# Dense pieces of elements 2 and 3 in halves, pieces spread by their length, and maxima twelve units ahead

## The chip, the cores and the metric

The kernel runs on one core of one Trainium2 chip. The metric is the device time of one execution in microseconds, from three executions of each kernel; lower is better. A separate execution was profiled, and every duration below comes from that one.

## The reference

Four elements of 1024 tokens with 256 channels pass through two layers. Each layer is attention and then a feed-forward part, and after each of the four there is a residual sum and a layer norm:

```python
x = _layernorm(x + _L0_attn_ref(x, ...))   # 16 heads of 16, q and k normalised and rotated, no mask
x = _layernorm(x + _L0_ffn_ref(x, ...))    # silu(x Wg^T) * (x Wu^T), then Wd; 768 hidden
x = _layernorm(x + _L1_attn_ref(x, ...))   # 8 heads of 32, causal
x = _layernorm(x + _L1_ffn_ref(x, ...))    # 16 experts, top 2, capacity 512
```

All matrix products are in float32. Both softmaxes subtract the row's maximum. For the first attention this is done as

```python
attn = jnp.einsum('bqhd,bkhd->bhqk', q, k)
attn = jax.nn.softmax(attn, axis=-1)
out = jnp.einsum('bhqk,bkhd->bqhd', attn, v)
```

## The kernel before

**Stages.** TensorE (PE) works through one long list of instructions whose order is written by hand. After a start-up part come: the first attention of element 0, the first attention of element 1, the second attention of element 0, the first attention of element 2, the second attention of element 1, the first attention of element 3, the second attentions of elements 2 and 3, and then the experts.

**The first attention in units.** The 16 heads of an element are four groups of four. A group has 16 units. In each unit `Attend.head` makes the scores of four heads (four matmuls of 32 rows that run side by side in the array, PE line 491), ScalarE (ACT) takes their exponential (line 500), and `Attend.values` multiplies the exponentials of the unit before with the values (PE line 509, "av"). The row maxima that the exponentials need are made one group ahead by `Maxima.head`: four more matmuls per unit (PE line 467), each reduced by VectorE (DVE, line 470). So `first_units` pairs unit i of group n with maxima unit i of group n+1: sixteen units ahead. Sixteen units of maxima of the very first group run alone, before the first attention of element 0 starts, and in the last group of element 3 there are no maxima left to pair with.

The eight score and maximum matmuls are issued as two fours, two of each kind in a four, and each needs one of the six PSUM banks of the pool `ps_s`. A bank comes free when ACT has taken its exponential or DVE has reduced it. The order on PE within a unit is: first four, the values of the unit before, for some units a transpose "pt" or "pto" of the heads' tiles, second four, and then the unit's place for other work.

**The other work.** `weave(units, n, pieces, ...)` puts a list of pieces into these places: the feed-forward part of layer 0 (`ffn0`), the projections for the second attention (`project1`), the output projections (`out_project0`, `out_project1`), the router (`route`). All of them write one PSUM bank, the only buffer of the pool `ps_m` (tag "m"), when `weave` is called with `big=False`, as it is in all first attentions; the "pt" and "pto" transposes use that bank too. In the second attentions `big=True`, and the pieces share the six banks of `ps_s`.

Before the change every piece counts alike: with 54 entries in the 64 units of element 2 an entry is issued where its number is due. Most dense pieces fill a whole bank, with eight matmul instructions of 256 columns (each product of two blocks is four matmul calls of two instructions). Shorter and longer ones are: a turn (four transposes), a router product "pl" (eight short instructions) and a down projection "dn" (twelve instructions). `second_end(b)` lists the output projection and router of element b, with entries `wait` that do nothing, so that some units stay empty there. Behind these come the rest of the feed-forward part and `project1`.

**Beside PE.** The bank of a piece is emptied as follows: a turn by one ACT copy of 512 columns (line 640), `gate_up` by an ACT tanh (664) and two DVE operations (665, 666), an output projection by two DVE additions in `add_residual` (556), `project1` by ACT copies (931, 935). Work with a delay (`later`) and the routing steps of `dispatch` are put on DVE and GpSimd (POOL) at the end of a unit, behind that unit's reductions and ahead of its piece. `dispatch` starts at unit 26 of the first attentions of elements 2 and 3, one step per unit.

Of the kernel before, what the change touches and what calls it, by code (L numbers as in the profile page):

```python
# [10 lines left out]
F32 = mybir.dt.float32  # L11
# [8 lines left out]
P = 128  # L20
# [6 lines left out]
FF0 = 768  # L27
# [8 lines left out]
def postln_layers_kernel(ctx: ExitStack, tc: tile.TileContext, a: dict, out: bass.AP):  # L36
# [75 lines left out]
    with ExitStack() as main:  # L112
# [179 lines left out]
        def project_v(b):  # L292
            def piece(j, big):
                xin = take_xin(b, j, "v") if b else xin0[j]
                ps = bank(f"v0_{b}_{j}", big)
                for i in range(2):
                    for c in range(2):
                        nc.tensor.matmul(
                            ps[:, i * 256 : (i + 1) * 256],
                            xin[:, c, i * P : (i + 1) * P],  # L300
                            w0[:, c, 512:768],
                            start=c == 0,
                            stop=c == 1,
                        )
                if b and xin_next:
                    load_ahead()
                nc.scalar.copy(va0[:, 2 * j : 2 * j + 2, :, 0:D0], ps.rearrange("p (t h d) -> p t h d", t=2, h=H0))

            return [lambda big, j=j: piece(j, big) for j in range(4)]

# [234 lines left out]

        def wait(big):
            pass

        mvs, rrs, open_rows = {}, {}, set()
# [33 lines left out]

        def project_out(b, j, oT, w, name, big):

            ps = bank(f"pp{name}_{b}_{j}", big)
            for i in range(2):
                for c in range(2):
                    nc.tensor.matmul(  # L589
                        ps[:, i * 256 : (i + 1) * 256], oT(c, i), w[:, c, :], start=c == 0, stop=c == 1  # L590
                    )
            for i in range(2):
                add_residual(b, 2 * j + i, ps[:, i * 256 : (i + 1) * 256], name)

        def out_project0(b):
# [21 lines left out]
            for h in range(2):  # L617
                out += [lambda big, h=h, c=c: turn(h, c, big) for c in range(2)]
                out += [lambda big, j=j: project(j, big) for j in (2 * h, 2 * h + 1)]
            return out  # L620

        def out_project1(b):


            def project(j, big):
                project_out(b, j, lambda c, i: oT1[b][:, c, (2 * j + i) * P : (2 * j + i + 1) * P], w1o, "a1", big)

            out = [lambda big, j=j: project(j, big) for j in range(4)]
            return out

# [12 lines left out]
        def ffn0(b):  # L643
# [4 lines left out]

            def gate_up(j, f, big):
                if f == 0:  # L650
                    hT[j] = act.tile([P, FF0 // P, 256], F32, tag="hT", bufs=1, name=f"hT_{b}_{j}")
                ps = bank(f"gu_{b}_{j}_{f}", big)
                for i, w in enumerate((wg, wu)):
                    for c in range(2):
                        nc.tensor.matmul(  # L655
                            ps[:, i * 256 : (i + 1) * 256],
                            w[:, c, f * P : (f + 1) * P],
                            xT[j][:, c, :],
                            start=c == 0,
                            stop=c == 1,  # L660
                        )

                sg = act.tile([P, 256], F32, tag="sg", bufs=1, name=f"sg_{b}_{j}_{f}")
                nc.scalar.activation(sg, ps[:, 0:256], AF.Tanh, scale=0.5)
                nc.vector.scalar_tensor_tensor(sg, sg, 1.0, ps[:, 0:256], ALU.add, ALU.mult)
                nc.vector.tensor_tensor(hT[j][:, f, :], ps[:, 256:512], sg, ALU.mult)

# [11 lines left out]

            out = [lambda big: turn(0, big)]  # L680
            for j in range(4):
                out += [lambda big, j=j, f=f: gate_up(j, f, big) for f in range(FF0 // P)]
                if j < 3:
                    out.append(lambda big, j=j: turn(j + 1, big))
                out += [lambda big, j=j, i=i: down(j, i, big) for i in range(2)]
            return out
# [9 lines left out]
        def route(b):  # L696
# [27 lines left out]
            tu, lo = [[lambda big, j=j, f=f: f(j, big) for j in range(4)] for f in (turn, logits)]  # L724
            return tu, lo

# [183 lines left out]
        def project1(b):  # L910
# [9 lines left out]

            def piece(j, s, big):
                ps = bank(f"p1_{b}_{j}_{s}", big)
                for i in range(2):
                    for c in range(2):
# [5 lines left out]
                if s == 2:  # L930
                    nc.scalar.copy(va1[b][:, 2 * j : 2 * j + 2, :].rearrange("p t c -> p (t c)"), ps)
                else:
                    for g in range(G1):
                        to = (qTs, kTs)[s][b, g][:, j * 256 : (j + 1) * 256]
                        nc.scalar.copy(to, ps[:, g * 256 : (g + 1) * 256])

            out = []
            for j in range(4):
                out.append(lambda big, j=j: turn(j, big))
                out += [lambda big, j=j, s=s: piece(j, s, big) for s in range(3)]  # L940
            return out
# [130 lines left out]

        groups = {}
        oq0, oT1, ends = {}, {}, {}

        def first_units(b):
# [3 lines left out]
            for g in range(G0):  # L1080
                n = 4 * b + g
                at = Attend(groups[n], oq0[b])
                mx = groups.get(n + 1)
                for i in range(16):
                    for hp in range(2):

                        then = []
                        for j in range(2):
                            if mx is not None:
                                then += [at.head(i, 2 * hp + j), mx.head(i, 2 * (1 - hp) + j)]  # L1090
                            elif hp == 0:
                                then += [at.head(i, 2 * j), at.head(i, 2 * j + 1)]
                        for fn in then:
                            fn()
                        if hp == 0:
                            if i > 0:
                                at.values(i - 1)
                            elif last is not None:
                                last.values(15)
                            if i == 3:  # L1100
                                groups[n].turn(0, 1, name="a")
                            if i == 5 and last is not None:
                                last.unload(1)
                            if i == 10 and mx is not None:
                                mx.turn(0, 0, name="a")
                            if i == 11:
                                at.unload(0)
                            if i >= 12 and n + 2 in groups:
                                groups[n + 2].turn((i - 12) // 2, i % 2)
                    if i == 0:  # L1110
                        groups[n].close(1)
                    if i == 3 and n + 2 < G0 * B:
                        nb, ng = divmod(n + 2, G0)
                        groups[n + 2] = Maxima(nb, ng)
                    if i >= 4 and n + 2 in groups:
                        groups[n + 2].rotate(4)
                    if i == 8 and mx is not None:
                        mx.close(0)
# [9 lines left out]
        def second_units(b):  # L1128
# [37 lines left out]
            at[last[0]].values(last[1])  # L1166

        def weave(units, n, pieces, big, mid=(), at=0, side=(), side_at=0, rate=1):


            mid, side = list(mid), list(side)
            done, total = 0, len(pieces) + len(mid)
            for u, _ in enumerate(units):
# [4 lines left out]
                if u >= at and mid:  # L1178
                    mid.pop(0)(big)
                    done += 1  # L1180
                    continue
                left = len(pieces)
                while left and (done < total * (u + 1) // n):
                    pieces.pop(0)(big)
                    done, left = done + 1, left - 1
            for piece in pieces:
# [112 lines left out]

        for k, i in enumerate((0, 2, 4, 6, 1, 3, 5, 7, *range(8, 16))):  # L1300
            for red in [groups[0].head(i, h) for h in range(4)]:
# [10 lines left out]
            if k == 10:  # L1312
                groups[0].turn(0, 0, name="a")
            if k >= 12:
                groups[1].turn((k - 12) // 2, k % 2, big=True)
            if 8 <= k < 12:
                second.pop(0)(True)
            else:
                early.pop(0)(False)
# [14 lines left out]

        def second_end(b):
            tu, lo = route(b)
            out = [wait] * 3 + out_project1(b) + [wait, tu[0], wait]
            return out + [lo[0], tu[1], wait, lo[1], tu[2], wait, lo[2], tu[3], wait, lo[3]]

# [10 lines left out]
        for b in (1, 2):  # L1350
# [10 lines left out]
                64,  # L1361
                second_end(b - 1) + ffn[cut:] + project1(b),
                False,
                [lambda big, b=b: load_heads(b + 2, 0)] if b + 2 < B else (),
                30,
                dispatch(b - 1, False),
                26,
            )
# [262 lines left out]
```

## Time and profile before

| | us |
|---|---|
| median of three executions | 2437.87 (2421.68 to 2438.58) |
| profiled execution, its own time | 2424.9 |
| its span, first to last instruction | 2423.2 |
| PE busy | 2300.8 (95% of the span) |
| DVE busy | 1380.2 (57%) |
| ACT busy | 1019.7 (42%) |
| POOL busy | 737.5 (30%) |

Busy times of PE overlap nothing but weight loads, but the ends of its matmuls are modelled, so a busy PE can still be waiting; the distance from one start to the next says more. In the rows of groups, a line stands for engine, source line, operation, tiles and shapes, count, busy time in us, mean ns of one, and the idle time of the engine before it with what ended it. In rows of the timeline the first two numbers are the start in us from the beginning of the span and the length.

### The profile page before, as it was taken

To read this page: it belongs to the slowest core of one execution; us is meant where nothing else is said; L and a number is where in the kernel's file an instruction comes from. 1 tells how busy PE (TensorE), PEld (TensorE's weight loads), DVE (VectorE), ACT (ScalarE), POOL (GpSimd) and SP (SyncE) were. 2 spreads that over 40 slices of the span, in tenths; PEclk is the share of its full clock that TensorE was granted. 3 is DMA by queue.
4 is the path that set the end of the run, shared out by engine and by line. 5 is a ranking of instruction groups with operands and counts; after the bars stand their busy time and mean duration, and the time that the engine had idled before them with its cause. 6 is when DMAs were issued, how large, how long until landed. Compare 5 with 4: busy or idle time off the path is not lost.

```text
span 2423.2 us, 36155 instructions
## 1 busy us (share of the span) xinstructions
PE 2300.8 (95%) x14004; PEld 1138.6 (47%) x14004; DVE 1380.2 (57%) x3231; ACT 1019.7 (42%) x2039; POOL 737.5 (30%) x1101
## 2 busy tenths in 40 slices
PE   8999999999999999999999999999999985999994
PEld 5333334444444443444444434445556443666662
DVE  7766766666557476776674767717645774111113
ACT  2565665555543445545434555562332331111112
POOL 5335337223205143253241420211112153222223
PEclk9999999999999999999999999998999886999997
DMA  3234111000000000000100000112000012444434
GB/s 104 62 120 138 59 59 51 1 28 1 1 28 1 1 1 24 5 27 27 54 1 1 1 1 12 36 46 80 1 1 1 1 58 92 96 107 107 106 88 150
DMA packets 78125, 107.78 MB, mean 44 GB/s; under 512 B 8832, under 2 KB 67200, under 8 KB 76288
## 3 DMA queue, kind: packets, MB, share of 16 engines
q1 hardware_dynamic: 48592, 73.34, 9.3%
q0 software_dynamic: 9984, 14.82, 3.2%
q10 hardware_dynamic: 19376, 17.30, 2.3%
q8 instruction: 110, 1.80, 0.3%
q14 instruction: 63, 0.52, 0.1%
HBM read 66.54 MB, written 38.90 MB: 44 GB/s over the span
## 4 chain that ended last, share of the span: by engine, by line
PE 87%; DVE 8%; DMA 1%; issue 1%; ACT 1%; POOL 1%; SPq 0%; DVEq 0%; POOLq 0%; ACTq 0%
PE sc L491 21%; PE av L509 10%; PE ph L1492 7%; PE py L1508 7%; PE gu L655 7%; PE mx L960 5%; PE sc L1010 4%; PE mx L467 4%; PE p L929 4%; PE dn L671 3%; PE av L1047 3%; PE ppa L589 3%; PE dn L1047 2%; DVE masked L970 2%; PE qk L321 2%; PE pt L458 1%
## 5 line engine op out<-in xcount | busy, mean ns | idle before, releaser
L470 DVE TENSOR_REDUCE part<-mx 128x1 f32<-128x512 f32 x1024 | 655.6, 684 | 305.8 <-PE mx L467 300.8
L500 ACT ACTIVATE pe<-sc 128x512 f32<-128x512 f32 x1024 | 554.2, 596 | 392.4 <-PE mx L467 349.2
L467 PE MATMUL mx<-kT,qT 32*128 32x512 f32 x2048 | 621.6, 637 | 0.2 <-DVE part L470 0.2
L491 PE MATMUL sc<-qT,kT 32*128 32x512 f32 x2048 | 604.3, 637 | 0.0
L491 PEld LDWEIGHTS sc<-qT,kT 32*128 32x128 f32 x2048 | 176.0, 183 | 218.3 <-issue 174.5
L509 PE MATMUL av<-pe,va 128*32 128x512 f32 x2048 | 272.9, 605 | 0.0
L1021 ACT ACTIVATE pe<-sc 128x512 f32<-128x512 f32 (+3 forms) x384 | 157.3, 496 | 202.2 <-PE sc L1010 202.0
L467 PEld LDWEIGHTS mx<-kT,qT 32*128 32x128 f32 x2048 | 186.1, 183 | 33.3 <-issue 16.0
L970 DVE CUSTOM_DVE_ANT_0 masked<-mx,mask_w 128x128 bf16<-128x128 f32 (+3 forms) x256 | 125.4, 490 | 111.7 <-PE mx L960 82.0
L1492 PE MATMUL ph<-dmT,f 128*128 128x512 f32 x384 | 170.4, 602 | 6.8 <-DVE dmT L100 3.5
L1500 ACT ACTIVATE hTm<-ph,b 128x512 f32<-128x512 f32 x96 | 60.8, 684 | 262.2 <-PE ph L1492 262.2
L1508 PE MATMUL py<-f,hTm 128*128 128x256 f32 x768 | 167.7, 379 | 0.0
L1512 POOL DMA_INDIRECT acc_d<-yo,dm x48 | 74.6, 1554 | 287.0 <-DVE yo L1510 243.8
L1508 PEld LDWEIGHTS py<-f,hTm 128*128 128x128 f32 x768 | 145.9, 190 | 25.0 <-issue 5.7
L1024 POOL TENSOR_SCALAR_AFFINE_SELECT pe<-pe 128x256 f32<-128x256 f32 x128 | 51.7, 412 | 313.2 <-ACT pe L1021 311.5
L960 PE MATMUL mx<-kT,qT 32*128 32x512 f32 (+3 forms) x768 | 138.6, 578 | 3.4 <-DVE x L556 2.7
L1509 DVE TENSOR_TENSOR yo<-py,b 128x256 f32<-128x256 f32 x48 | 20.4, 425 | 213.1 <-PE py L1508 213.1
L386 POOL TENSOR_TENSOR ss<-ss,neg_half 128x16 f32<-128x16 f32 x48 | 139.3, 2910 | 0.5
L509 PEld LDWEIGHTS av<-pe,va 128*32 128x32 f32 x2048 | 40.4, 108 | 192.5 <-issue 186.4
L1010 PE MATMUL sc<-qT,kT 32*128 32x512 f32 (+3 forms) x768 | 123.7, 550 | 5.2 <-ACT pe L1021 1.5
L1492 PEld LDWEIGHTS ph<-dmT,f 128*128 128x128 f32 x384 | 72.9, 192 | 97.4 <-issue 86.8
L856 POOL DMA_INDIRECT disp_d<-row,si x48 | 48.4, 1009 | 221.6 <-DVE row L845 215.4
(350 smaller groups left out, 2992.7 us busy)
## 6 DMA issues: line engine op xcount, KB each, us to landing
f<-in_fc SPq DMA_DIRECT2D x14, 1024.0 KB, 5.0
f<-in_fc ACTq DMA_DIRECT2D x10, 1024.0 KB, 5.9
disp_d<-empty ACTq DMA_DIRECT2D x12, 520.0 KB, 3.3
xink<-in_xT SPq DMA_DIRECT2D x24, 256.0 KB, 3.0
qk_d<-xs SPq DMA_DIRECT2D x6, 1024.0 KB, 5.1
xr<-qk_d SPq DMA_DIRECT2D x6, 1024.0 KB, 6.0
dm<-disp_d SPq DMA_DIRECT2D x11, 520.0 KB, 3.6
x<-in_x SPq DMA_DIRECT2D x32, 128.0 KB, 2.7
```

The source lines that it names most:

```text
L467: nc.tensor.matmul(sc, self.qT[r, t * P : (t + 1) * P], self.kT[r, u * 512 : (u + 1) * 512], start=True, stop=True)
L470: return lambda: nc.vector.tensor_reduce(self.part[:, t, u, h : h + 1], sc, AX.X, ALU.max, negate=True)
L491: nc.tensor.matmul(sc, self.m.kT[r, kt * P : (kt + 1) * P], self.m.qT[r, qb * 512 : (qb + 1) * 512], start=True, stop=True)
L500: nc.scalar.activation(self.pes[i, h // 2][:, h % 2, :], sc, AF.Exp)
L509: nc.tensor.matmul(self.av[32 * h : 32 * h + 32, :], va0[:, kt, 4 * self.g + h, :], self.pes[i, h // 2][:, h % 2, :], start=kt == 0, stop= ...
L655: nc.tensor.matmul(ps[:, i * 256 : (i + 1) * 256], w[:, c, f * P : (f + 1) * P], xT[j][:, c, :], start=c == 0, stop=c == 1,)
L960: nc.tensor.matmul(scs[h][:, :n], qT[r, t * P : (t + 1) * P], kT[r, u * 512 : u * 512 + n], start=True, stop=True,)
L970: nc.vector.tensor_tensor_reduce(masked[:, :n], scs[h][:, :n], mask_w[:, 512 - n :], -1.0, -NEG, ALU.add, ALU.min, part)
L1010: nc.tensor.matmul(scs[h][:, off:], ones_h[r, :] if w else kT[r, kt * P : (kt + 1) * P], (self.m.nmT if w else qT)[r, q], start=w == 0, st ...
L1021: nc.scalar.activation(pe[:, j, off:], scs[2 * hp + j][:, off:], AF.Exp)
L1492: nc.tensor.matmul(ph[:, i * CAP : (i + 1) * CAP], f1[:, c, (f + i) * P : (f + i + 1) * P], dmT[:, c, :], start=c == 0, stop=c == 1,)
L1508: nc.tensor.matmul(py[:, :C], hT[:, f, c * P : (c + 1) * P], f2[:, f, :], start=f == 0, stop=f == FF1 // P - 1)
```

## The change

1. Pieces get a cost: 2 for a whole dense piece, 1 for a half, 3 for a down projection, 0.75 for a turn or a router product. `weave` spreads them by cost in place of number, over all its calls that have pieces of such costs: the first attention of element 1 and the second attentions too. The element that loads heads no longer takes a piece's place.
2. `project_out`, `gate_up` and `project1`'s `piece` can be done in halves (`whole`, `in_halves`): one half makes 256 columns of the bank, with four matmul instructions, and is emptied on its own. Only `second_end` asks for halves, so only the first attentions of elements 2 and 3 have them. The entries `wait` are gone there; halves of the feed-forward part stand between the steps of the output projection and the router.
3. `LEAD = 12`: the maxima are twelve units ahead. Twelve units of maxima run alone at the start, and the last four of a group are paired with the first four units of its own attention. The turns and rotations that belong to a maxima unit move with it.
4. `dispatch` starts at unit 25.

The new places on PE in the first attention of element 2: 74 pieces in 64 units, 16 units with two pieces and 6 with none. Before: 46 pieces, one unit with two and 19 with none. For element 3: before 18 units without a piece (2 of them among the 16 units without maxima), after 6, and 18 units in whose place more than one user of the bank follows another, 5 of them among the 12 units without maxima (there the "pto" and "pt" transposes stand in the same place as the pieces).

```diff
+        def whole(fn, *args):
+            def piece(big):
+                fn(*args, big, (0, 1))
+            piece.halves = [lambda big, k=k: fn(*args, big, (k,)) for k in range(2)]
+            piece.cost = 2.0
+            return piece
+
+        def in_halves(pieces):
+            return [h for p in pieces for h in getattr(p, "halves", [p])]
...
-            def gate_up(j, f, big):
+            def gate_up(j, f, big, ks):
...
-                ps = bank(f"gu_{b}_{j}_{f}", big)
-                for i, w in enumerate((wg, wu)):
+                ps = bank(f"gu_{b}_{j}_{f}_{ks[0]}", big)
+                for i in ks:
...
-                sg = act.tile([P, 256], F32, tag="sg", bufs=1, name=f"sg_{b}_{j}_{f}")
-                nc.scalar.activation(sg, ps[:, 0:256], AF.Tanh, scale=0.5)
-                nc.vector.scalar_tensor_tensor(sg, sg, 1.0, ps[:, 0:256], ALU.add, ALU.mult)
-                nc.vector.tensor_tensor(hT[j][:, f, :], ps[:, 256:512], sg, ALU.mult)
+                if 0 in ks:
+                    sgs[j] = sg = act.tile([P, 256], F32, tag="sg", bufs=1, name=f"sg_{b}_{j}_{f}")
+                    nc.scalar.activation(sg, ps[:, 0:256], AF.Tanh, scale=0.5)
+                    nc.vector.scalar_tensor_tensor(sg, sg, 1.0, ps[:, 0:256], ALU.add, ALU.mult)
+                if 1 in ks:
+                    nc.vector.tensor_tensor(hT[j][:, f, :], ps[:, 256:512], sgs[j], ALU.mult)
...
+        LEAD = 12
...
                 at = Attend(groups[n], oq0[b])
-                mx = groups.get(n + 1)
                 for i in range(16):
+                    k, j = divmod(16 * n + i + LEAD, 16)
+                    mx = groups.get(k)
                     for hp in range(2):
                         then = []
-                        for j in range(2):
+                        for h in range(2):
                             if mx is not None:
-                                then += [at.head(i, 2 * hp + j), mx.head(i, 2 * (1 - hp) + j)]
+                                then += [at.head(i, 2 * hp + h), mx.head(j, 2 * (1 - hp) + h)]
...
-            done, total = 0, len(pieces) + len(mid)
+            done, total = 0.0, sum(map(cost, pieces))
...
                 if u >= at and mid:
                     mid.pop(0)(big)
-                    done += 1
-                    continue
-                left = len(pieces)
-                while left and (done < total * (u + 1) // n):
-                    pieces.pop(0)(big)
-                    done, left = done + 1, left - 1
+                while pieces and done + cost(pieces[0]) / 2 < total * (u + 1) / n:
+                    piece = pieces.pop(0)
+                    piece(big)
+                    done += cost(piece)
...
-        for k, i in enumerate((0, 2, 4, 6, 1, 3, 5, 7, *range(8, 16))):
+        for k, i in enumerate((0, 2, 4, 6, 1, 3, 5, 7, *range(8, LEAD))):
...
-        def second_end(b):
+        def second_end(b, fill):
             tu, lo = route(b)
-            out = [wait] * 3 + out_project1(b) + [wait, tu[0], wait]
-            return out + [lo[0], tu[1], wait, lo[1], tu[2], wait, lo[2], tu[3], wait, lo[3]]
+            o, f = in_halves(out_project1(b)), in_halves(fill)
+            out = o[:2] + f[:1] + o[2:4] + f[1:2] + o[4:6] + f[2:3] + o[6:] + f[3:5]
+            for j in range(4):
+                out += [tu[j], f[5 + j], lo[j]]
+            return out + f[9:]
...
-                second_end(b - 1) + ffn[cut:] + project1(b),
+                second_end(b - 1, ffn[cut:] + project1(b)),
```

## The prediction

> **What bounds the kernel now.** I read the page first: PE is busy for 95% of the span, the others are far below.
>
> ```profile
> span 2423.2 us, 36155 instructions
> ...
> PE 2300.8 (95%) x14004; PEld 1138.6 (47%) x14004; DVE 1380.2 (57%) x3231; ACT 1019.7 (42%) x2039; POOL 737.5 (30%) x1101
> ...
> L470 DVE TENSOR_REDUCE part<-mx 128x1 f32<-128x512 f32 x1024 | 655.6, 684 | 305.8 <-PE mx L467 300.8
> L500 ACT ACTIVATE pe<-sc 128x512 f32<-128x512 f32 x1024 | 554.2, 596 | 392.4 <-PE mx L467 349.2
> ```
>
> DVE's reductions and ACT's exponentials mostly wait for PE. Per unit they are 4 x 0.684 = 2.74 and 4 x 0.596 = 2.38 us. Next the busy times by stage: the last of the start-up (four maxima units alone), the first attention of element 2, that of element 3.
>
> ```profile
> 59.50:71.90 12.40, 12.23 (x65) 6.75 (x64) 11.96 (x22) 4.55 (x10) 0.00 (x0) 1.00 0.13 43
> ...
> 860.40:1177.90 317.50, 315.10 (x2013) 134.70 (x2007) 223.22 (x452) 174.54 (x331) 118.85 (x182) 1.00 0.05 18
> ...
> 1335.00:1631.60 296.60, 291.98 (x1865) 125.18 (x1857) 182.06 (x391) 168.00 (x324) 66.42 (x124) 1.00 0.05 15
> ```
>
> The columns are length, then PE, weight loads, DVE, ACT, POOL, then the granted clock. In the start-up DVE is the full engine (11.96 of 12.40), in the attentions PE. But "busy" hides waits, so I took PE's timeline and measured from "av" to "av", which is one unit. First a unit whose place holds a half piece, then one whose place is empty:
>
> ```profile
> 144.35 1.06 PE L509 MATMUL av<-pe,va 128*32 128x512 f32 x8
> ...
> 146.42 1.13 PE L321 MATMUL qk<-w,xink 128*128 128x256 f32 x4
> 147.48 0.69 PE L491 MATMUL sc<-qT,kT 32*128 32x512 f32 x1
> ...
> 148.55 1.07 PE L509 MATMUL av<-pe,va 128*32 128x512 f32 x8
> ...
> 152.55 1.06 PE L509 MATMUL av<-pe,va 128*32 128x512 f32 x8
> ```
>
> The half (start 146.42, next four at 147.48) costs 1.06 us and its unit 4.20. The empty unit that follows takes 4.00, only 0.2 less: with nothing between them the two fours need eight banks of six, and the second waits for a reduction. A whole piece:
>
> ```profile
> 1054.02 1.07 PE L509 MATMUL av<-pe,va 128*32 128x512 f32 x8
> ...
> 1056.08 1.13 PE L655 MATMUL gu<-xTf,wg 128*128 128x256 f32 x4
> 1057.05 1.03 PE L655 MATMUL gu<-xTf,wu 128*128 128x256 f32 x4
> 1058.01 0.69 PE L491 MATMUL sc<-qT,kT 32*128 32x512 f32 x1
> ...
> 1059.08 0.64 PE L509 MATMUL av<-pe,va 128*32 128x512 f32 x4
> ```
>
> It costs 1058.01 - 1056.08 = 1.92 us, its unit 5.06. In the same way: a turn alone 0.59, unit 3.99 (free in an otherwise empty unit); a down projection 2.79, unit 5.92; "pt" or "pto" adds 0.59. A unit is thus 3.14 us (1.07 + 1.07 + 1.00) plus its piece; an empty one loses 0.85, one with a lone turn 0.27. These numbers rebuild the stage of element 2 within 4 of its 317.5 us.
>
> **Halves, the gain.** Whole plus empty is 9.05 us, two units of one half 8.40. Element 2 goes from 19 empty units to 6 (-13 x 0.85 = -11.1) and from 9 lone turns to 2 (-7 x 0.27 = -1.9).
>
> **Halves, their price.** The Trainium skill (page "TensorEngine Tiling (Array Packing)", Key Properties) says that a change of tiling mode drains TensorE, which speaks against this change: halves double the number of passages from 32-row tiles to the full array and back. It gives no price; the rows do. Eight instructions at 0.216 us (their start-to-start here) are 1.73, the whole piece takes 1.92; four are 0.86, the half 1.06. So a passage costs 0.2 us: 28 split pieces x 0.2 = +5.6 per element, and by the bare count of instructions it would be nothing. I take the rows.
>
> **Two pieces in one place.** The costs of element 2 sum to about 78 in 64 units, so 16 units get two pieces, and all pieces write the one bank of `ps_m`. PE's list is in order: the second piece waits until the first is emptied, and everything behind it, the next four, "av" and then ACT and DVE, waits too. Before there is one such unit in element 1, two down projections, with its wait in the timeline:
>
> ```profile
> 524.01 2.86 PE L671 MATMUL dn<-wd,hT 128*128 128x256 f32 x12
> ...
> 526.91 0.43 DVE L556 TENSOR_TENSOR x<-dn,x 128x256 f32<-128x256 f32 x1 [1.48 <-PE dn L671]
> ...
> 527.39 2.86 PE L671 MATMUL dn<-wd,hT 128*128 128x256 f32 x12 [0.52 <-DVE x L556]
> ```
>
> It lost 3.38 - 2.79 = 0.59. For the others I measured, on single pieces of before, how long after PE's next start the bank was emptied. A turn: the copy runs behind two exponentials,
>
> ```profile
> 909.77 0.66 PE L639 MATMUL ptxn<-ident,x 128*128 128x128 f32 x4
> ...
> 910.88 0.59 ACT L640 COPY xTn<-ptxn 128x512 f32<-128x512 f32 x1
> ```
>
> and ends at 911.47, 1.12 after the 910.35 at which the turn was over. The first `gate_up` half needs tanh and then a DVE operation: 0.94 (mean 1.16). The second half, or an output projection's, needs one DVE operation behind the unit's two reductions, about 0.9. A `project1` half is one ACT copy of 0.375, ready 0.5 after. Element 2 has as first of two: 6 turns (6.7), 3 first `gate_up` halves (2.8), a second half and an output projection (1.8), 4 `project1` (2.0): 13.3 us; the routing positions share a place before as well. Bounds: nothing, if the copies were done in time, which the 0.59 above excludes as a rule; and twice as much for the DVE-emptied ones beside `dispatch` (units 25 on), whose steps DVE takes before the piece: at 1043.30 a `gate_up` was over and its DVE operation ran only at 1045.19. I add 2.5 for three such units. Element 2 together: -13.0 + 5.6 + 13.3 + 2.5 = +8.4.
>
> **Element 3, same pieces.** Empty units with maxima 16 to 6 (-8.5), lone turns 6 to 2 (-1.1), two empty ones without maxima lose 0.27 each (-0.5), passages +5.6. Doubled places with maxima: 5 turns (5.6), the same 4.6 for the DVE-emptied ones, 2 `project1` (1.0) and 2.5 beside `dispatch`, 13.7; without maxima 5 against 3 before, +2. Sum +11.2.
>
> **Maxima twelve ahead.** Four units leave the start-up: -12.4 (first row of the stages). Their work reappears beside the last group of element 3, four fours of 1.07 and four "pt" of 0.59: +6.6. Their four half pieces fill empty units in element 0: 4 x 0.2 = +0.8. The re-turn of q now stands one unit before its use; ACT's copy of 0.59 has about 2 us for that, so nothing. Net -5.0. Element 3 with its four units: +17.8.
>
> **The other weaves.** Element 1 keeps whole pieces, but a cost of 0.75 now puts five pairs into one place: 3 more empty units (+2.6), 6 lone turns fewer (-1.6), waits 5.0 against 1.4 for the pairs of before: +4.6. In the second attentions heavier pieces come earlier, about 4 us of PE work by the middle, into the stretch where PE waits for DVE's masked reductions; the banks are six there. Bounds: -4 each (all hidden) and +2 (additions ahead of reductions on DVE). I take -5 for the three. `dispatch` one unit earlier, rotations four later on POOL, and the loads of heads on SP's queue at the same unit 30: their users are units away, nothing; if POOL were late, a normalisation would hold DVE for about 0.7 each time, as single units of 5.80 in place of 5.06 show.
>
> **Sum.** -12.4 + 0.8 + 4.6 + 8.4 + 17.8 - 5 = +14.2 us. On the profiled execution, 2424.9, that is 2439. That execution lies 0.5% below the median of the three, 2437.9, which the forecast is for: 2452.
>
> **Rivals.** (a) As summed, between about -24 and +24, or 1%, which is about what a measurement of this kernel can tell from no change: 0.56. (b) Slower by more: the single bank of `ps_m`. If DVE-emptied doubles wait for `dispatch` and for `later` work everywhere as at 1043.30, about 1.9 us in place of 0.9, and if half units of 4.2 us leave DVE, at 3.5 to 3.8 us per unit beside `dispatch`, too little slack, some 14 doubles and 30 half units lose 0.5 to 1 more: +15 to +25, so 2467 to 2477. It decides, that is passes 1%, from 10 us over my sum, about 0.7 us per DVE-emptied double. For it: PE can't pass the wait. Against: ACT-emptied doubles are the majority. 0.34. (c) Faster: the waits are covered, because a second four that would have stalled anyway finds its banks free; then the 36 us of double waits (15.8 + 15.7 + 5.0) fall to half and the second attentions give 4 each: 14 - 18 - 7 = -11, 2427, and with all covered 2409. For it: an empty unit shows 0.85 of such cover. Against: a place with a turn and a half already lasts longer than that. Below -1%: 0.10.
>
> The range takes in most of (b) and the likelier end of (c).
>
> **What the profile after would show.** Half units at 4.20; units with a turn and a half at about 5.9 and PE rows with "<-ACT xTn" or "<-DVE sg" before the second piece; the stage of element 2 at about 326, of element 3 at 314, the first "av" about 12 us earlier. I am wrong if doubles lose under 0.3 us, if half units exceed 4.5 in the mean, or if the granted clock, 0.95 to 0.96 in the second attentions, changes there.

## The result and the profile after

The changed kernel takes 2458.1 us, median of four executions (2456.35 to 2460.26); the kernel before, 2430.68 (2421.68 to 2438.58; four executions, three of them those that the forecast stood on). The ratio is 1.0122 with a 95% interval of 1.0089 to 1.0154. It is slower: the whole interval lies above 1, most of it above 1.01. The profiled execution went from 2424.9 to 2456.35, 31.4 us more; the sum had said 14.2. The 2458 us lie inside the range that the prediction describes, 6 above its 2452 and below the 2467 to 2477 of rival (b).

The page of the changed kernel, the lines that answer those shown of before:

```profile
span 2454.6 us, 36232 instructions
...
PE 2291.4 (93%) x14004; PEld 1110.4 (45%) x14004; DVE 1383.9 (56%) x3231; ACT 1021.3 (42%) x2049; POOL 737.3 (30%) x1101
...
L470 DVE TENSOR_REDUCE part<-mx 128x1 f32<-128x512 f32 x1024 | 657.1, 685 | 339.5 <-PE mx L467 334.9
L500 ACT ACTIVATE pe<-sc 128x512 f32<-128x512 f32 x1024 | 554.5, 595 | 455.2 <-PE mx L467 422.8
```

PE has the same 14004 instructions and 9 us less of busy time in a span that is 31 us longer: it waits more. DVE's and ACT's waits for PE's scores grew with it (305.8 to 339.5, 392.4 to 455.2), so neither of these two has become the full engine. Busy times by stage, columns as in the prediction: the first attention of element 2, that of element 3.

```profile
851.90:1184.30 332.40, 314.40 (x2008) 124.13 (x2004) 225.04 (x451) 174.05 (x335) 119.85 (x183) 0.99 0.05 18
1339.80:1659.10 319.30, 298.81 (x1896) 118.13 (x1888) 191.66 (x403) 170.11 (x330) 65.87 (x124) 0.99 0.04 14
```

Element 2 took 317.4 and takes 332.4; PE's busy time there is the same (315.1 to 314.4), so the 15 us are waits, or PE running slower. DVE is at 225 of 332. The granted clock, 1.00 in these two stages before, is 0.99 now; what that is worth is told below.

Lengths of all stages in us, each from its first to the next stage's first start on PE, with the runs that follow (the experiments name them):

| | start-up | el. 0 | el. 1 | 2nd att. 0 | el. 2 | 2nd att. 1 | el. 3 | 2nd att. 2+3 | rest |
|---|---|---|---|---|---|---|---|---|---|
| before | 71.9 | 288.8 | 342.7 | 157.1 | 317.4 | 157.2 | 295.1 | 408.5 | 384.5 |
| changed | 59.1 | 292.0 | 347.2 | 153.6 | 332.4 | 155.5 | 319.3 | 411.4 | 384.0 |
| forecast of the difference | -12.4 | +0.8 | +4.6 | (-5 with the other two) | +8.4 | | +17.8 | | 0 |
| difference | -12.8 | +3.2 | +4.5 | -3.5 | +15.0 | -1.7 | +24.2 | +2.9 | -0.5 |
| one per place | 61.0 | 291.5 | 341.4 | 153.5 | 308.6 | 155.9 | 296.4 | 407.3 | 383.9 |
| second on six | 59.4 | 291.5 | 343.9 | 153.4 | 315.5 | 158.5 | 300.9 | 409.6 | 383.9 |
| piece first | 61.0 | 291.3 | 347.2 | 158.6 | 329.5 | 158.5 | 315.5 | 409.1 | 383.8 |
| dispatch late | 59.2 | 291.3 | 347.2 | 153.6 | 329.6 | 155.9 | 312.5 | 411.7 | 384.1 |
| whole, even | 60.8 | 291.9 | 341.4 | 153.5 | 317.5 | 153.5 | 300.9 | 416.6 | 384.0 |
| LEAD only | 59.3 | 294.2 | 342.1 | 159.2 | 317.1 | 157.7 | 301.4 | 418.2 | 383.7 |
| one per place, LEAD 16 | 71.8 | 287.2 | 342.3 | 158.5 | 309.6 | 153.5 | 289.3 | 408.6 | 384.1 |
| one per place, piece first | 60.9 | 291.8 | 341.4 | 153.5 | 308.7 | 155.7 | 295.0 | 412.3 | 383.8 |
| one per place, dispatch late | 59.4 | 292.0 | 341.4 | 155.8 | 312.1 | 155.7 | 294.5 | 409.3 | 383.8 |

**Where the misses lie.** I went through the changed kernel's units of elements 2 and 3, from "av" to "av", and took off the prediction's own price list: 3.14 for the unit, 0.59 for a "pt" or a turn, 1.06 for a half, 2.79 for a down projection (and, from units of these runs, 0.99 for a router product, 1.30 for the routing positions). What is left is loss:

| loss in us | doubled places | single pieces (beyond the 0.27 of a lone turn) | empty beyond 0.85 |
|---|---|---|---|
| before, element 2 | 1 with positions: 1.2 | 2.3 | 0.6 |
| changed, element 2 | 16: 22.4 (priced 15.8) | 40: 3.6 | 0.0 |
| changed, element 3, with maxima | 13: 20.2 (priced 13.7) | 32: 3.7 | 0.0 |

Of the misses of these two stages, 6.6 and 6.4 us, the doubled places are 5.4 (22.4 - 1.2 - 15.8) and about 6. Single pieces lose 1.3 more than before in element 2. In each stage 3.2 us of these losses are not waiting but PE's clock, as shown below. An ordinary doubled place, in the changed kernel's timeline (a turn, then a `gate_up` half; columns start, length, engine, line, operation, and in brackets the wait before):

```profile
919.08 1.07 PE L509 MATMUL av<-pe,va 128*32 128x512 f32 x8
...
921.15 0.66 PE L653 MATMUL ptxn<-ident,x 128*128 128x128 f32 x4
...
921.29 1.08 ACT L500 ACTIVATE pe<-sc 128x512 f32<-128x512 f32 x2 [1.04 <-PE mx L467]
922.26 0.59 ACT L654 COPY xTn<-ptxn 128x512 f32<-128x512 f32 x1
922.91 1.13 PE L671 MATMUL gu<-xTf,wg 128*128 128x256 f32 x4 [1.11 <-ACT xTn L654]
...
925.04 1.07 PE L509 MATMUL av<-pe,va 128*32 128x512 f32 x8
...
1008.71 1.13 PE L671 MATMUL gu<-xTf,wg 128*128 128x256 f32 x4
...
1009.88 0.38 ACT L681 ACTIVATE sg<-gu 128x256 f32<-128x256 f32 x1
1010.05 0.28 DVE L822 TENSOR_TENSOR lg<-oh 128x128 f32<-128x128 f32 x1
...
1012.12 0.18 DVE L830 TENSOR_TENSOR si<-pk,none_f 128x16 int32<-128x16 f32 x1
1012.22 0.41 DVE L682 SCALAR_TENSOR_TENSOR sg<-sg,gu 128x256 f32<-128x256 f32 x1
1012.68 1.13 PE L671 MATMUL gu<-xTf,wu 128*128 128x256 f32 x4 [2.84 <-DVE sg L682]
...
1013.75 1.22 PE L491 MATMUL sc<-qT,kT 32*128 32x512 f32 x1
```

The first unit takes 5.96, as forecast (5.9): the half waits for the turn's copy, which runs behind two exponentials. The second part is an extraordinary place. The tanh of the first half is over at 1010.26, but ten small DVE operations of one `dispatch` step, issued at 1010.05 to 1012.12, stand ahead of the one that empties the bank; PE waits 2.84, and the unit takes 9.29.

Not all of this is waiting. The score matmul at 1013.75 takes 1.22, where 0.69 is usual in these timelines. These are PE's busy time and clock just ahead of it and from there on:

```profile
1010.30:1013.70 3.40, 1.01 (x4) 0.68 (x4) 2.09 (x11) 0.00 (x0) 0.00 (x0) 1.00 0.00 0
1013.70:1017.10 3.40, 3.40 (x17) 0.71 (x16) 1.63 (x3) 1.08 (x2) 0.00 (x0) 0.50 0.02 5
```

For 3.4 us the granted clock is half. The same happens from 1003.5, and twice in element 3 (from 1491.6 and 1501.8); before, no stretch of these two stages has it. Each of the four follows 3.4 us in which PE was busy for 1.0 to 1.4. Against the same instructions elsewhere, the two spells cost 1.4 us in the unit at 997.63, 1.1 in the one shown and 0.6 in the one behind it, 3.2 in all, and in element 3 as much.

Of the 22.4 us in element 2, thirteen ordinary doubles lost 12.4 (priced 11.4): 1.17 behind a turn, 0.53 where ACT empties a `project1` half, 1.0 to 1.14 where DVE does. Three places lost 10.0: 2.62 in the unit at 861.85 (the second piece waits behind two reciprocals of `later`, 1.75 us, line 1088), 3.34 at 997.63 (positions and a half), 4.03 at 1006.47 (the one shown); 2.5 of the 10.0 are the half clock. Element 3 has the same three places with 2.62, 3.24 and 4.14.

### The profile page after: what moved, and what is told of

Its sections match the earlier page's. It is cut to its first block, busy times and chain, and to the rows that moved or that the text cites. A ratio compares the mean times of both kernels' runs of the same rounds, so it can differ in the third digit from the quotient of the medians.

```text
span 2454.6 us, 36232 instructions
## 1 busy us (share of the span) xinstructions
PE 2291.4 (93%) x14004; PEld 1110.4 (45%) x14004; DVE 1383.9 (56%) x3231; ACT 1021.3 (42%) x2049; POOL 737.3 (30%) x1101
## 4 chain that ended last, share of the span: by engine, by line
PE 84%; DVE 10%; ACT 2%; issue 2%; DMA 1%; POOL 1%; SPq 0%; DVEq 0%; POOLq 0%; ACTq 0%
PE sc L491 21%; PE av L509 10%; PE ph L1521 7%; PE py L1537 7%; PE gu L671 6%; PE sc L1033 4%; PE mx L983 4%; PE p L948 4%; PE dn L689 4%; PE av L1070 3%; DVE masked L993 3%; PE mx L467 3%; PE dn L1070 2%; PE qk L321 2%; PE ppa L604 2%
## 5 line engine op out<-in xcount | busy, mean ns | idle before, releaser
L470 DVE TENSOR_REDUCE part<-mx 128x1 f32<-128x512 f32 x1024 | 657.1, 685 | 339.5 <-PE mx L467 334.9
L500 ACT ACTIVATE pe<-sc 128x512 f32<-128x512 f32 x1024 | 554.5, 595 | 455.2 <-PE mx L467 422.8
L467 PE MATMUL mx<-kT,qT 32*128 32x512 f32 x2048 | 610.8, 642 | 0.1
L491 PE MATMUL sc<-qT,kT 32*128 32x512 f32 x2048 | 594.4, 642 | 0.8 <-ACT pe L500 0.8
L491 PEld LDWEIGHTS sc<-qT,kT 32*128 32x128 f32 x2048 | 166.1, 183 | 222.1 <-issue 180.2
L467 PEld LDWEIGHTS mx<-kT,qT 32*128 32x128 f32 x2048 | 174.0, 183 | 19.8 <-issue 8.8
L983 PE MATMUL mx<-kT,qT 32*128 32x512 f32 (+3 forms) x768 | 131.8, 560 | 9.4 <-DVE x L553 6.8
L1033 PE MATMUL sc<-qT,kT 32*128 32x512 f32 (+3 forms) x768 | 129.9, 563 | 3.7 <-ACT w_3a L789 1.5
L671 PE MATMUL gu<-xTf,wg 128*128 128x256 f32 x384 | 108.6, 405 | 12.8 <-DVE hT L684 4.9
L671 PE MATMUL gu<-xTf,wu 128*128 128x256 f32 x384 | 102.7, 390 | 15.9 <-DVE sg L682 7.5
```

Of the source, the lines that this page charges most:

```text
L467: nc.tensor.matmul(sc, self.qT[r, t * P : (t + 1) * P], self.kT[r, u * 512 : (u + 1) * 512], start=True, stop=True)
L470: return lambda: nc.vector.tensor_reduce(self.part[:, t, u, h : h + 1], sc, AX.X, ALU.max, negate=True)
L491: nc.tensor.matmul(sc, self.m.kT[r, kt * P : (kt + 1) * P], self.m.qT[r, qb * 512 : (qb + 1) * 512], start=True, stop=True)
L500: nc.scalar.activation(self.pes[i, h // 2][:, h % 2, :], sc, AF.Exp)
L671: nc.tensor.matmul(ps[:, i * 256 : (i + 1) * 256], (wg, wu)[i][:, c, f * P : (f + 1) * P], xT[j][:, c, :], start=c == 0, stop=c == 1,)
L983: nc.tensor.matmul(scs[h][:, :n], qT[r, t * P : (t + 1) * P], kT[r, u * 512 : u * 512 + n], start=True, stop=True,)
```

## Experiments

Theory: the slowdown is the waits for the single bank, ordinary ones at every doubled place and long ones at the three where DVE is busy. Rivals: the halves themselves (more passages, more DVE and ACT work to a unit), the order of `dispatch` on DVE, or the twelve units ahead. Each run was measured beside before on one chip; there were three sessions, each on another chip. The median of before was 2421.71 for the first four, 2435.67 for the next three and 2433.29 for the last two, so I read the stages of the table first, and medians against ratios.

### One piece to a place

```diff
-            o, f = in_halves(out_project1(b)), in_halves(fill)
+            o, f = in_halves(out_project1(b)), in_halves(fill[:20]) + fill[20:]
...
-            done, total = 0.0, sum(map(cost, pieces))
+            length = (lambda piece: 1.0) if even else cost
+            done, total = 0.0, sum(map(length, pieces))
```

with `even=True` in the first attentions of elements 1, 2 and 3: 18 of 28 pieces are halved, so that all entries fit into the 64 places, and each counts alike.

> The changed kernel, but only 18 of the 28 dense pieces of elements 2 and 3 are halved, so that their pieces are 63 for 64 places and none has two; element 1 spreads by number again. Theory (two pieces in one place wait for the one bank, and that is what the change loses): the first attention of element 2 falls from 332.5 us to about 306 (317.4 before, 18 empty places of 0.85 filled, 18 passages of 0.2 added), that of element 3 from 319.3 to about 293, element 1 from 347.2 to 342.5; together 2398, about 1.1% under the kernel before. Rival (halves themselves cost more than 0.2 each, because units of 4.2 us leave DVE no slack beside the routing steps): element 2 at 314 to 318, element 3 at 302 to 306, 2415 to 2425.

Measured: 2405.92 (2400.18 to 2415.32), ratio 0.9932 (0.9901 to 0.9963).

```profile
847.40:1156.00 308.60, 305.56 (x2008) 123.11 (x2004) 223.15 (x451) 173.55 (x331) 120.08 (x183) 1.00 0.06 20
1311.90:1608.30 296.40, 290.67 (x1895) 116.48 (x1888) 192.20 (x403) 169.26 (x326) 66.10 (x124) 0.99 0.05 15
```

Element 2 falls from 332.4 to 308.6 and element 3 from 319.3 to 296.4, by 23.8 and 22.9, with LEAD and the early `dispatch` still in place. For element 2 the parts are: 21.1 less loss in doubled places, five empty units (4.3) and ten passages (2.0) fewer, and against these 2.1 more loss in single pieces and six more lone turns (1.6): 23.7. The half clock is gone from element 2 and down to one spell of 3.4 us in element 3. This version beats both kernels: the change is worth making without the doubled places.

### The second piece of a place on other banks

```diff
-                    piece(big)
+                    piece(big or here > 0)
+                    here += 1
```

in the changed kernel: of several pieces in a place the second and later take a bank of the six of `ps_s`. Nothing else moves.

> The changed kernel with one edit: in a place with more than one piece the second one writes a bank of the pool of six in place of the only bank of the other pool, so it does not wait for the first to be emptied. Theory (the one bank): places with two pieces lose their waits, about 20 us each in elements 2 and 3 and 4 in element 1; the bank that it borrows costs the next four up to 0.5 each (some 17 in all), so 2456 falls by 25 to 40, to 2416 to 2431. Rival (what is lost is the passages between tilings and DVE time, which stay): within 6 us of 2456.

Measured: 2416.18 (2412.41 to 2423.37), ratio 0.9963 (0.9937 to 0.9989). The same turn and half as above:

```profile
911.23 1.06 PE L509 MATMUL av<-pe,va 128*32 128x512 f32 x8
...
913.30 0.66 PE L653 MATMUL ptxn<-ident,x 128*128 128x128 f32 x4
913.79 1.03 PE L671 MATMUL gu<-xTf,wg 128*128 128x256 f32 x4
...
915.82 1.06 PE L509 MATMUL av<-pe,va 128*32 128x512 f32 x8
```

The half starts 0.49 after the turn, before the turn's copy has even begun, and the unit takes 4.59 in place of 5.96. Loss in doubled places falls from 22.4 to 6.1 in element 2, and the stages by 16.9, 18.4 and, in element 1, 3.3. Order, halves and work being equal, this shows that most of the waits are for the one bank. (About 2.0 of the 16.3 are something else: in ten places the two pieces now follow each other without a wait and share a passage of 0.2, which bears out its price.) The largest loss left is 3.84, in the unit with the positions: these are a step of `dispatch` and still use the one bank, and 1.9 of it is half clock (989.2 to 996.0). Two turns still lose 1.17 each, as in the changed kernel:

```profile
1061.00 0.66 PE L653 MATMUL ptxa<-ident,x 128*128 128x128 f32 x4
...
1062.76 1.13 PE L948 MATMUL p<-xTa,w1q 128*128 128x256 f32 x4 [1.11 <-ACT xTa L654]
```

Here the second piece reads the very tile `xTa` that the turn's copy makes. It waits for its data, and no bank can help.

### The piece ahead of the step of `dispatch`

```diff
+                for _ in range(rate if u >= side_at and first else 0):
+                    if side:
+                        side.pop(0)()
```

behind the pieces instead of ahead of them (`first=True` for elements 2 and 3).

> The changed kernel with one edit: in the first attentions of elements 2 and 3 the unit's piece is issued before its routing step, so that on DVE the operation that empties the bank stands ahead of the step's. Theory (the waits beside the routing steps, such as 2.84 us in the place with two halves of gate_up in unit 28, are DVE's queue): element 2 falls from 332.5 to 326 or 327, element 3 from 319.3 to 313 or 314, the total by about 12 us to 2444. Rival (the wait is set by the unit's reductions and the chain tanh, then DVE): less than 3 us in all.

Measured: 2455.41, ratio 1.0126 (1.0075 to 1.0177): a miss in the total. The stages gained only 2.9 and 3.8, and the second attentions of elements 0 and 1 took 5.0 and 3.0 more, at a lower clock (last section). In element 2 the doubled places beside `dispatch` fell from 8.5 to 3.6 us of loss, as meant. But an empty unit of 3.99 now takes 5.18, and single halves lose more too: some of the wait moves one unit on. Of the 2.9 and 3.8, up to 1.7 and about 3.2 are the half clock, of which one spell is left in element 2 and none in element 3. Order on DVE is a smaller part than I expected.

### `dispatch` beside pieces that ACT empties

```diff
-                25,
+                44,
...
+                for _ in range((rate if u < side_at + 6 or side_at < 40 else 3) if u >= side_at else 0):
```

(Units in this expectation are counted from one, the step 25 or 44 in the code from zero.)

> The changed kernel with dispatch moved from unit 25 to unit 44 in elements 2 and 3 (six units with one step each, then three steps to a unit), where the pieces are projections of the second attention, which ACT empties. In the changed kernel the doubled units 28 and 29 of each element lose 3.3 and 4.1 in place of 1.0, single halves beside dispatch 2.6 together. Theory (DVE-emptied pieces queue behind dispatch on DVE, and these few places are the part of the slowdown that was not in the sum): doubles fall to about 1 each, elements 2 and 3 each faster by 6 to 8, to about 325 and 312, total 2441 to 2445. Rival (dispatch takes DVE and POOL time that PE pays for wherever it stands): the loss moves to units 44 to 60, both stages within 2 us, total 2455.

Measured: 2445.31 (2442.9 to 2448.92), ratio 1.0075 (1.0051 to 1.0099). The two `gate_up` halves of the long place:

```profile
1004.11 1.13 PE L671 MATMUL gu<-xTf,wg 128*128 128x256 f32 x4
...
1005.70 0.42 DVE L682 SCALAR_TENSOR_TENSOR sg<-sg,gu 128x256 f32<-128x256 f32 x1 [0.17 <-ACT sg L681]
1006.17 1.13 PE L671 MATMUL gu<-xTf,wu 128*128 128x256 f32 x4 [0.93 <-DVE sg L682]
```

0.93 in place of 2.84: without `dispatch` the long place is an ordinary one. Element 3, whose last units have no maxima for DVE, gains 6.8, the size that the theory gives; about 3.2 of it is the half clock, which is gone there. Element 2 gains only 2.8: `project1` halves beside three steps to a unit lose 4.2 there, and the unit with the reciprocals lost 4.25 in this run, with a spell of half clock from 867.6. So `dispatch` costs PE something wherever DVE also reduces maxima; the theory holds for the long waits and the rival for about half of the sum in element 2.

### No halves, even spread

One piece to a place as before, but `second_end` asks for no halves:

```diff
-            o, f = in_halves(out_project1(b)), in_halves(fill[:20]) + fill[20:]
-            out = o[:2] + f[:1] + o[2:4] + f[1:2] + o[4:6] + f[2:3] + o[6:] + f[3:5]
+            o, f = out_project1(b), fill
+            out = o + f[:3]
             for j in range(4):
-                out += [tu[j], f[5 + j], lo[j]]
-            return out + f[9:]
+                out += [tu[j], lo[j], f[3 + j]]
+            return out + f[7:]
```

> One piece to a place as in the run before of that kind, LEAD 12, but no piece is halved: all dense pieces of elements 2 and 3 are whole, spread evenly, so element 2 has 18 empty places in place of 1, element 3 has 14 with maxima and 3 without. Theory (halves are worth their length where they do not double a place: whole plus empty 9.05 against 8.40): 0.65 for each of the 17 and 13 places, so element 2 about 308.6 + 11 = 320, element 3 about 296.4 + 9 = 305, total 2405.9 + 20 = 2426, as slow as before. Rival (halves give nothing, the whole gain of the run with one piece to a place lies in the even spread): element 2 at 308, element 3 at 297, total 2406.

Measured: 2419.47 (2403.78 to 2424.78), ratio 0.9933 (0.9901 to 0.9966), but against a before of 2435.67.

```profile
847.60:1165.10 317.50, 315.00 (x2010) 132.86 (x2007) 223.55 (x451) 174.43 (x331) 120.08 (x183) 1.00 0.06 19
```

Element 2 stands at 317.5, where it was before the change (317.4): the spread alone gives nothing. Halving 18 pieces gives 8.9 and 4.5 us, against 11 and 9 expected. In element 2 the shortfall is the halves of `gate_up` at the start of `dispatch` and of the output projection: 7.1 us of loss with halves, 4.8 without.

### Maxima twelve ahead, alone and taken back

The kernel before with LEAD = 12 and the start-up of the changed one, nothing else; and one piece to a place with

```diff
-        LEAD = 12
+        LEAD = 16
...
+            if k >= 12:
+                groups[1].turn((k - 12) // 2, k % 2, big=True)
-            if 8 <= k:
+            if 8 <= k < 12:
```

> The kernel before with the maxima twelve units ahead and nothing else of the change. Theory: the start-up is 12.8 us shorter, element 0 longer by 1 to 3, elements 1 and 2 as before (342.7 and 317.4), element 3 longer by 6.6 (301.7): 3 to 5 us less in all, 2420 to 2422 against a profiled 2425. Rival (the shorter lead makes the attention wait for the re-turned q or the last reductions): elements 1 and 2 longer by 2 us or more each, and no gain in all.

> One piece to a place, 18 halves, but the maxima sixteen units ahead as before. Prediction's own sum for LEAD 12 was -12.4 + 0.8 + 6.6 = -5, so this should be at 2411: start-up about 73, element 0 at 290.7, element 3 about 290. Rival, after the run that did LEAD alone (element 0 slower by 3 to 5 in every kernel with LEAD 12, from a table load and a wait for a transfer on ACT that 16 units ahead do not show): element 0 at 288.8, total 2407 or less, so that LEAD 12 is worth nothing.

Measured: 2431.1 (2424.21 to 2434.58), ratio 1.0017 (0.9988 to 1.0046), and 2405.93 (2401.06 to 2412.07), ratio 0.9884 (0.9841 to 0.9928), against 2405.92 with 12 ahead. Start-up 12.6 shorter and 10.8 longer; element 3 6.3 longer and 7.1 shorter (priced 6.6); element 0 5.4 longer and 4.3 shorter (priced 0.8). Twelve ahead is worth about nothing. (LEAD alone has a half-clock spell of 3.4 us in element 0, from 197.1, so up to 1.7 of its 5.4.) What element 0 loses stands in ACT's timeline of the changed kernel:

```profile
69.74 1.28 ACT L258 ACT_TABLE_LOAD   x1 [0.46 <-DVE ss L257]
...
71.62 1.28 ACT L500 ACT_TABLE_LOAD   x1
...
194.62 0.37 ACT L337 COPY xs<-qk 128x256 f32<-128x256 f32 x1 [2.92 <-DMA qk_d<-xs]
```

There are four units fewer ahead of it, so the square root of line 258, which in the kernel before stands in the start-up at 66.32 with no table load, falls between exponentials: two table loads of 1.28, and its unit takes 6.50 in place of 4.79. And a copy waits 2.92 for the transfer that reads its buffer, where no such wait in element 0 of the kernel before exceeds 2.04; the exponentials behind it wait too, and that unit takes 6.13 in place of 4.20. Together 3.6 us.

### The best version, further

One piece to a place with the piece first, and with `dispatch` from unit 44: the same edits as above.

> One piece to a place, 18 halves, LEAD 12, and in elements 2 and 3 the piece is issued ahead of the step of dispatch. In the run without this last edit single halves beside dispatch took 5.3 to 7.6 in place of 4.2 to 4.8, an excess of about 6 us in each of the two elements. Theory (the piece's emptying queues behind the step's operations on DVE): element 2 falls from 308.6 to about 303 to 305, element 3 from 296.4 to about 290 to 293, total 2395 to 2400. Rival (the excess is DVE's work itself, which only moves to the next unit): both stages within 1 us, total 2406.

> One piece to a place, 18 halves, LEAD 12, dispatch from unit 44 as in the run before this one. In the same kernel with dispatch at 25 units 26 to 28 lost 4.6 in element 2 and 5.9 in element 3. Theory: element 2 falls from 308.6 to about 304, element 3 from 296.4 to about 291, total 2396. Rival: nothing, 2405; or worse, if three steps to a unit hold DVE's maxima: above 2406.

Measured: 2403.79 (2398.22 to 2405.91), ratio 0.9868 (0.9827 to 0.991), and 2400.59 (2399.4 to 2405.58), ratio 0.9878 (0.9837 to 0.9919). Both stages moved by +0.1 and -1.4 in the first, +3.5 and -1.9 in the second. In absolute times all four versions with one piece to a place lie between 2400.59 and 2405.93, and their ratios differ mostly because before did. Both theories missed. Half clock covers nearly all that moved: the second run has 6.8 us of it in element 2 (from 1072.1), worth 2.8; the version that they start from has 3.4 in element 3, worth 1.6, where these two have none. So where no place is doubled, the 4 to 6 us at the start of `dispatch` stay whatever the order; that they are DVE's own work is the likeliest reading.

## Why the prediction was right or wrong

- **Right: what bounds.** The 31 us are mostly PE's waits, at unchanged counts and nearly unchanged busy time.
- **Right: start-up, element 1, the price of units.** -12.8 (-12.4), +4.5 (+4.6). Half units are at 4.20, turn and half at 5.96, down projections at 5.92. The passage of 0.2 stands: with it the price list gives the times of undisturbed half units to 0.01.
- **Mis-sized: "Two pieces in one place", "I add 2.5 for three such units".** The mechanism was right and the wait is for the bank (the run on six banks). The ordinary doubles were right within 1 us in 12.4. The three in which DVE has other work lost 10.0 in element 2, 2.5 of it at half clock. They were priced at about 4.4 (2.5, and 0.94 for the first half in two of them), and at nothing more for the positions than the 1.2 that they lost before: 4.4 too little. (The 2.5 were meant for three places beside `dispatch`; one of these was ordinary, and one that was not stands beside reciprocals instead.) The ordinary ones add 1.0, together 5.4 of the stage's 6.6. Most of the rest is single pieces, a term that the sum did not have. The bound from above was "twice as much"; one place took four times 0.94, about 1.1 us of that at half clock. The row at 1043.30 had the rest of a normalisation and one operation of `dispatch` ahead on DVE; the doubled place met ten operations. Two of the six turns wait for data and not for the bank, at the same price.
- **Put at nothing: PE's clock in these stages.** The prediction looked for a change of the clock in the second attentions only. Of the misses of 6.6 and 6.4, 3.2 each are the half clock behind the long waits.
- **Mis-sized: "re-turn of q ... so nothing" and "+0.8" for element 0.** The steps that LEAD moves with the maxima were looked at for their users, not for ACT's table and the transfers of `rotate`: +3.2, of which two units account for 3.6. "Net -5.0" for LEAD came out near 0.
- **Not borne out: "I take -5 for the three" second attentions.** The prediction's own sign came up, a changed clock there: 0.95 before and 0.98 in the changed kernel in that of element 0. They gave -2.3 in the changed kernel, and the clock moves each of the first two by up to 5 (below). At the same granted clock, 0.96, the spread by cost takes 155.5 to 155.9 where before has 157.2; at 0.94 there is 158.5 against 157.7 and 159.2. So about -1 each for the first two at best, and nothing that can be told for the third.
- **Rival (a)**, the likeliest by its chance of 0.56, did not come: +27.4 is beyond its 24, though the interval, from about +22 on, still touches it. **Rival (b)** had the sign, the bank and about the size (the profiled execution came out 17.2 over the sum, (b) said 15 to 25), but not the way there: not all DVE-emptied doubles wait 1.9. Most lose 1.0 to 1.14, and three places 2.6 to 4.1. **Rival (c)** is out: no doubled place with a turn or a DVE-emptied piece first was covered.
- **The median.** The forecast stood on 2437.87; with one more execution before's median is 2430.68. The median rose by 27.4, about twice the forecast difference, but the forecast time is off by 6 only, since its base lay 7.2 higher. That closeness is luck. A small slip beside it: the row of element 3 before (296.60) ends 1.4 past the stage's end, so its forecast of 314 should read 313.

## What to carry to other kernels

Filling an empty slot of an in-order engine with a second user of the same single buffer costs the buffer's emptying time, and can cost more than the slot was worth: here an empty unit lost 0.85, a doubled place 0.5 to 4.1. So price a doubled place by what stands ahead of the emptying operation in its engine's queue at that very place, not by a mean. Cut pieces only until they fill the slots one to one, or give the second user another buffer, which helps wherever it does not need what the first one makes: that turned +1.2% into -0.7% and -0.4%. Count the clock, too: four of the long waits here were followed by 3.4 us at half of it. A lead or an offset that moves a whole bundle of steps moves their table loads and transfers too.

## What the runs showed of the hardware

The second attentions of elements 0 and 1 have the same work in every one of these kernels with the spread by cost, yet their lengths fall on few values, and the granted clock goes with them. The same stage in the changed kernel, columns as before, and the next fence in the kernel with the piece first:

```profile
698.30:851.90 153.60, 144.58 (x1092) 73.19 (x1088) 91.87 (x268) 53.58 (x126) 46.42 (x63) 0.98 0.04 13
```

```profile
699.50:858.10 158.60, 150.23 (x1093) 76.09 (x1092) 92.04 (x269) 53.68 (x126) 46.31 (x63) 0.94 0.04 11
```

Over nine runs: 153.4 to 153.6 at a clock of 0.97 to 0.98, 155.5 to 155.9 at 0.96, 158.5 to 158.6 at 0.94; in the stage of elements 2 and 3, 407.3 at 0.89 and, with the pieces spread by number, 418.2 at 0.86. The first attentions run at 0.99 to 1.00.

These means hide that the clock has two values in the traces, 1 and 0.5, the second in spells of 3.4 us or a multiple. Taken from the traces' clock records, in us at half clock:

| | 2nd att. 0 | el. 2 | 2nd att. 1 | el. 3 |
|---|---|---|---|---|
| before | 17.1 | 0 | 13.7 | 0 |
| changed | 6.8 | 6.8 | 13.7 | 6.8 |
| one per place | 6.8 | 0 | 13.7 | 3.4 |
| second on six | 6.8 | 6.8 | 20.5 | 3.4 |
| piece first | 20.5 | 3.4 | 20.5 | 0 |
| dispatch late | 10.2 | 3.4 | 13.7 | 0 |

So in the nine runs 153.4 to 153.6 go with 6.8 or 10.2 us at half clock, 155.5 to 155.9 with 13.7 and 158.5 to 158.6 with 20.5. In elements 2 and 3 of the changed kernel the spells come right behind long waits of PE, but that is not so everywhere: before, the one from 760.1 follows 3.4 us in which PE was busy throughout. What sets their number in an execution stays open.

Two such stages at the two ends make 10 us, 0.4% of the kernel. Single runs of before in the first session fall into two groups, 2416 to 2427 at a mean clock of 0.964 to 0.971 and 2433 to 2440 at 0.959 to 0.960. That the second attentions make them is likely but wasn't shown, since only profiled executions list the clock by stage.
